# Reciprocals of softmax sums: spread by VectorE and turned by one transpose, in place of narrow products

## The chip, the cores and the metric

The kernel runs on one core of a Trainium2 chip. The metric is the device time of one execution in microseconds. Profiles are one execution each, recorded by the hardware profiler.

## What is computed

A block with two layers: each is a gated cross-attention to a context, followed by a gated feed-forward part. x has 16 batch rows of 100 tokens with 512 features; the context has 16 rows of 722 tokens with 384 features. Everything is float32. The part that matters here is the attention, once with 16 heads of 32 features (attention 0), once with 8 heads of 64 (attention 1):

```python
q = (query @ Wq + bq).reshape(B, Nq, H, D).transpose(0, 2, 1, 3)
k = (key_value @ Wk + bk).reshape(B, Nkv, H, D).transpose(0, 2, 1, 3)
v = (key_value @ Wv + bv).reshape(B, Nkv, H, D).transpose(0, 2, 1, 3)
attn = jnp.einsum('bhqd,bhkd->bhqk', q, k) * scale
attn = jax.nn.softmax(attn, axis=-1)
x = jnp.einsum('bhqk,bhkd->bqhd', attn, v).reshape(B, Nq, Cq)
return x @ Wo + bo
...
x = x + jnp.tanh(g_xattn[0]) * _L0_xattn_ref(_layernorm(x, axis=-1), ctx_768, ...)
x = x + jnp.tanh(g_ffn[0]) * _L0_ffn_ref(_layernorm(x, axis=-1), ...)
x = x + jnp.tanh(g_xattn[1]) * _L1_xattn_ref(_layernorm(x, axis=-1), ctx_768, ...)
x = x + jnp.tanh(g_ffn[1]) * _L1_ffn_ref(_layernorm(x, axis=-1), ...)
```

The first feed-forward part is a mixture of eight experts, the second has quantized weights. Neither is touched by the change.

## The kernel before

The kernel goes through attention 0, routing and experts, attention 1 and the quantized feed-forward part one after the other. Both attentions are the class `Attention`, with D = 32 or 64 features a head.

**Chunks.** Within an attention the work goes by batch row b (16) and by slice m of 128 features (4). One such pair, 64 in an attention, is called a chunk here; it holds G = 128 / D heads, that is four in attention 0 and two in attention 1. A chunk passes through these steps:

- `scores`: the products of queries and keys, tile `ps_s` (100 queries by 361 keys, two halves), line 315. VectorE negates them out of PSUM and takes the row minimum as it goes (`ns`, L338 with four heads in two parts, L325 with two heads); with four heads `extremes` (L348) joins the halves.
- `softmax`: ScalarE's exponentials (`pr`, L357), which also sum each row into `sums`.
- `turn`: TensorE transposes the probabilities of a pair of heads, four 100x128 blocks into one bank `ps_t` (L374), three banks a turn. The three are copied to `pT` by ScalarE (L381) or VectorE (L383), alternating by `(m + pair + q) % 2`. Four heads have two turns a chunk (turn 0 and turn 1), two heads one.
- `attend`: the reciprocal of `sums` (`rinv`, L390); the narrow products `ps_r` (L393), one for each head, whose weights are one column of `rinv` repeated D times and whose moving operand is the identity, so that `ps_r` holds each head's reciprocals along the queries in all its D feature rows; the copy `rb` of it (L401); the weighted sums of the values `ps_pv` (L406); and the product of `ps_pv` with `rb` into `tT` (L413). It comes one chunk later than the chunk's turns.

Between these stand "units" of other work for TensorE, one bank each: keys (`ps_k`, L181) and values (`ps_v`, L203) of the next batch row, queries (`ps_q`, L275), input transposes (`ps_tr`, L129), output projections (`ps_y`, L419), and in attention 0 the experts' `ps_logits` (L567).

**What sets the order.** TensorE's order is written out by hand in `run`. In step i it is: `scores` of the next chunk (part 0), `attend` of the chunk before, some units, turn 0 of this chunk, some units, and with four heads also `scores` part 1 of the next chunk, turn 1, and the rest of the units. The order on VectorE, ScalarE and GpSimd is set by a scheduler from the program's dependencies and its own costs.

**Buffers.** [...] `ps_s` takes four of them, and all the rest (`ps_k`, `ps_v`, `ps_q`, `ps_tr`, `ps_y`, `ps_logits`, `ps_t`, `ps_r`, `ps_pv`) share the pool `ps_m` of four banks. A tile of this pool gets a bank when the tile that held it has been copied out. `rinv` and `rb` have two buffers each.

Of the kernel before, what the change touches and what calls it, by code (L numbers as in the profile page):

```python
# [8 lines left out]
F32 = mybir.dt.float32  # L9
# [7 lines left out]
P = 128  # L17
B, T, C = 16, 100, 512
# [31 lines left out]
def bcast(ap, *shape):  # L50
    return ap.to_broadcast(list(shape))
# [6 lines left out]
def tiles_for(b):  # L58

    return [i for i in range(NTT) if (i * P + rows_of(i) - 1) // T == b]  # L60
# [72 lines left out]
class Attention:  # L133
# [232 lines left out]
    def turn(self, b, m, pair):  # L366
# [16 lines left out]
                nc.vector.tensor_copy(to, ps)  # L383
        self.pT[b, m, pair] = t

    def attend(self, b, m):
        nc, D, G = self.net.nc, self.D, self.G

        rinv = self.p2.tile([T, G], F32, tag="rinv", name="rinv")
        nc.vector.reciprocal(rinv, self.sums[b][:, m * G : (m + 1) * G])  # L390
        ps_r = self.ps_m.tile([P, T], F32, tag="mm", name="ps_r")
        for j in range(G):
            nc.tensor.matmul(  # L393
                ps_r[j * D : (j + 1) * D, :],
                bcast(rinv[:, j : j + 1], T, D),
                self.net.ident[:T, :T],
                start=True,
                stop=True,
            )
        rb = self.p2.tile([P, T], F32, tag="rb", name="rb")  # L400
        nc.vector.tensor_copy(rb, ps_r)  # L401
        ps = self.ps_m.tile([P, T], F32, tag="mm", name="ps_pv")
        for c in range(NS):
            n = P if c < NS - 1 else SL
            for j in range(G):
                nc.tensor.matmul(  # L406
                    ps[j * D : (j + 1) * D, :],
                    self.v[b][:n, c, m * P + j * D : m * P + (j + 1) * D],
                    self.pT[b, m, j // 2][:n, j % 2 * NS + c, :],
                    start=(c == 0),  # L410
                    stop=(c == NS - 1),
                )
        nc.vector.tensor_tensor(self.tT[:, m, b * T : (b + 1) * T], ps, rb, ALU.mult)  # L413
# [18 lines left out]
    def run(self, given, after_project=None):  # L432


        parts = 2 if self.G == 4 else 1
        steps = [(b, m) for b in range(B) for m in range(KC)]
        last_tile = lambda g: ((g + 1) * GT - 1) // P
        extra = {i: [] for i in range(len(steps) + 40)}
        for g in range(1, B // GB):
            at = 4 * KC * (g - 1)  # L440
            for n, i in enumerate(range(last_tile(g - 1) + 1, last_tile(g) + 1)):
                extra[at + 2 + n].append((self.query_input, i))
            for m in range(KC):
                extra[at + 7 + 2 * m].append((self.queries, g, m))
        for b in range(B):
            for i in tiles_for(b):
                at = (b + 1) * KC + 1
                extra[at].append((self.project, i))
                for later, *unit in after_project(i) if after_project else ():
                    extra[at + later].append(tuple(unit))  # L450
        todo = [u for b in range(1, B) for u in self.keys_and_values(b)]
        for i, (b, m) in enumerate(steps):
            if m == 0 and b + 2 < B and b + 2 not in self.cxs:
                self.load_ctx(b + 2)

            upto = max(0, min(len(todo), int(3.5 * (i + 1) - 2)))
            units = extra[i] + todo[given:upto]
            given = max(given, upto)
            nxt = steps[i + 1] if i + 1 < len(steps) else None
            if nxt:  # L460
                self.scores(*nxt, 0)
            if i:
                self.attend(*steps[i - 1])
            n = len(units)
            cut = [0, (n + 1) // 2, n] if parts == 1 else [0, (2 * n + 4) // 5, (3 * n + 4) // 5, n]
            for f, *a in units[cut[0] : cut[1]]:
                f(*a)
            self.turn(b, m, 0)
            for f, *a in units[cut[1] : cut[2]]:
                f(*a)  # L470
            if parts == 2:
                if nxt:
                    self.scores(*nxt, 1)
                self.turn(b, m, 1)
                for f, *a in units[cut[2] :]:
                    f(*a)
            if nxt:
                self.softmax(*nxt)
        self.attend(*steps[-1])
        for i in range(len(steps), len(steps) + 40):  # L480
            for f, *a in extra[i]:
                f(*a)
# [976 lines left out]
```

## Time and profile before

| | us |
|---|---|
| median of 3 runs | 2925.89 (2925.71 to 2926.7) |
| the profiled execution's own time | 2935.15 |
| its span, from first to last instruction | 2933.4 |
| TensorE (PE) busy | 2819.8 |
| VectorE (DVE) busy | 869.2 |
| ScalarE (ACT) busy | 855.2 |
| the narrow products ps_r: 512 matmul records in attention 0, 256 in attention 1 | busy 24.2 and 25.3 |
| the reciprocals at L390, 128 | busy 21.8 |
| the copies rb at L401, 128 | busy 32.9 |

How to read it: a float32 product leaves two matmul records, a transpose one. Records of matmuls overlap and their ends are modelled, so the distance from one start to the next tells what a product costs; "busy" counts overlaps once. PEld is the loading of weights, which mostly runs beside matmuls. In tables by shape, "128x400 f32<-128x400 f32" is what is written and what is read. "idle before <-" names what ended the idle time of an engine ahead of a group. Attention 0's chunks run from about 85 to 975 us of the span, attention 1's from about 1730 to 2500.

### The profile page before, as it was taken

What the parts mean: (1) busy time and instruction counts of PE and PEld (TensorE: products, weight loads), DVE (VectorE), ACT (ScalarE), POOL (GpSimd) and SP (SyncE); (2) the same over time, 40 slices, a digit from 0 to 9 for tenths busy, and PEclk for the clock granted to TensorE, in tenths of its full rate; (3) what the DMA queues carried; (4) which work ended last, traced back from release to release, by engine and by line L of the source; (5) the groups of instructions that cost most, each with busy time, mean ns of one, the idle gap of its engine ahead of it and who ended that gap; (6) DMA issues with size and microseconds to landing.
All of it is one profiled execution on the core that took longest, in us unless ns stands there. A gap on an engine that the chain in (4) does not pass through costs nothing. (4 is left out here: it accounts for less than half of the span.)

```text
span 2933.4 us, 42386 instructions
## 1 busy us (share of the span) xinstructions
PE 2819.8 (96%) x17968; PEld 1746.7 (60%) x17968; DVE 869.2 (30%) x2565; ACT 855.2 (29%) x1710; POOL 149.2 (5%) x170
## 2 busy tenths in 40 slices
PE   7999999999999989999999979999999999499999
PEld 3555555555556578887888645555555556245543
DVE  2544444444445400000000163232232223410000
ACT  1544444454455300000000123333333333111110
POOL 2000000000000000000000140000000000210000
PEclk9999999999999999999999979999999999799999
DMA  4000010000000388889888420000000000700000
GB/s 155 16 16 16 18 37 24 16 27 32 16 27 21 137 320 315 314 323 318 312 316 313 153 64 31 16 31 16 16 31 16 31 16 1 225 8 11 11 11 13
DMA packets 131240, 278.10 MB, mean 95 GB/s; under 512 B 6880, under 2 KB 6880, under 8 KB 130528
## 3 DMA queue, kind: packets, MB, share of 16 engines
q1 hardware_dynamic: 111168, 231.19, 22.4%
q10 hardware_dynamic: 15328, 29.14, 3.0%
q0 software_dynamic: 4544, 14.95, 1.4%
q8 instruction: 145, 2.38, 0.3%
q14 instruction: 55, 0.45, 0.1%
HBM read 260.31 MB, written 14.94 MB: 94 GB/s over the span
## 5 line engine op out<-in xcount | busy, mean ns | idle before, releaser
L203 PE MATMUL ps_v<-wv_a,ctx_a 128*128 128x512 f32 (+1 forms) x1152 | 524.5, 600 | 7.6 <-ACT v_a L210 5.2
L181 PE MATMUL ps_k<-ctx_a,wk_a 128*128 128x361 f32 x1536 | 510.0, 477 | 14.4 <-DMA ctx_a<-in_ctxT 10.9
L774 PE MATMUL ps_h<-xT,w 128*128 128x128 f32 x3712 | 421.0, 276 | 0.9 <-DVE xT L762 0.9
L774 PEld LDWEIGHTS ps_h<-xT,w 128*128 128x128 f32 x3712 | 418.4, 193 | 1.8 <-DVE xT L762 1.3
L181 PEld LDWEIGHTS ps_k<-ctx_a,wk_a 128*128 128x128 f32 x1536 | 283.2, 192 | 174.1 <-issue 28.3
L203 PEld LDWEIGHTS ps_v<-wv_a,ctx_a 128*128 128x128 f32 (+1 forms) x1152 | 204.6, 185 | 243.8 <-issue 228.2
L338 DVE TENSOR_SCALAR_CACHE_REDUCE ns<-ps_s 100x361 f32<-100x361 f32 x512 | 246.9, 529 | 208.2 <-PE ps_s L315 185.8
L374 PEld LDWEIGHTS ps_t<-ident,pr_a 100*128 100x128 f32 x2304 | 214.0, 141 | 81.0 <-issue 41.7
L357 ACT ACTIVATE pr_a<-ns,extremes 100x722 f32<-100x722 f32 x256 | 227.2, 889 | 78.9 <-DVE extremes L348 78.9
L374 PE MATMUL ps_t<-ident,pr_a 100*128 100x100 f32 x2304 | 237.1, 252 | 1.5 <-DVE rb L401 1.1
L383 DVE COPY pT<-ps_t 128x400 f32<-128x400 f32 x288 | 163.7, 572 | 251.6 <-PE ps_t L374 245.6
L315 PE MATMUL ps_s<-kT_a,qT_a 32*100 32x361 f32 (+1 forms) x1536 | 213.6, 501 | 9.9 <-DVE ns L325 7.4
L210 ACT COPY v_a<-ps_v 128x512 f32<-128x512 f32 x192 | 111.3, 581 | 340.7 <-PE ps_v L203 340.4
L794 PE MATMUL ps_o<-w,midT 128*128 128x512 f32 x464 | 203.9, 592 | 0.0
L977 PE MATMUL ps_z<-ffn_w,y_ffn 128*128 128x512 f32 (+1 forms) x416 | 195.5, 607 | 5.4 <-ACT y_ffn L967 5.4
L325 DVE TENSOR_SCALAR_CACHE_REDUCE ns<-ps_s 100x722 f32<-100x722 f32 x128 | 111.4, 907 | 278.2 <-PE ps_s L315 278.2
L959 PE MATMUL ps_y<-hT,ffn_w 128*128 128x384 f32 (+1 forms) x512 | 188.9, 513 | 0.0
L381 ACT COPY pT<-ps_t 128x400 f32<-128x400 f32 x288 | 141.5, 492 | 158.8 <-PE ps_t L374 149.4
L315 PEld LDWEIGHTS ps_s<-kT_a,qT_a 32*100 32x100 f32 (+1 forms) x1536 | 73.7, 162 | 141.6 <-issue 92.6
L406 PE MATMUL ps_pv<-pT,v_a 128*32 128x100 f32 (+3 forms) x4608 | 156.6, 249 | 0.4 <-DVE pT L383 0.3
L785 DVE TENSOR_TENSOR midT<-silu,ps_h 128x512 f32<-128x512 f32 x58 | 39.9, 688 | 386.0 <-PE ps_h L774 386.0
L959 PEld LDWEIGHTS ps_y<-hT,ffn_w 128*128 128x128 f32 x512 | 98.2, 195 | 90.8 <-issue 52.9
(149 smaller groups left out, 1804.8 us busy)
## 6 DMA issues: line engine op xcount, KB each, us to landing
w<-in_L_ffn_w SPq DMA_DIRECT2D x116, 1024.0 KB, 7.1
w<-in_L_ffn_wo SPq DMA_DIRECT2D x29, 2048.0 KB, 11.0
ctx_a<-in_ctxT SPq DMA_DIRECT2D x30, 1083.0 KB, 5.2
q<-in_L_ffn_fc_q SPq DMA_DIRECT2D x8, 1024.0 KB, 10.8
s<-in_L_ffn_fc_scales ACTq DMA_DIRECT2D x8, 1024.0 KB, 12.4
rows<-ot ACTq DMA_DIRECT2D x29, 256.0 KB, 8.7
x<-in_x ACTq DMA_DIRECT2D x1, 3072.0 KB, 20.6
xn_d<-xn_moe ACTq DMA_DIRECT2D x12, 256.0 KB, 2.0
```

The source lines that it names most:

```text
L181: nc.tensor.matmul(ps, self.wk[:, k, m * P : (m + 1) * P], self.cxs[b][:, k, c * SH : (c + 1) * SH], start=(k == 0), stop=(k == KK - 1),)
L203: nc.tensor.matmul(ps[:n], self.cxs[b][:, k, c * P : c * P + n], self.wv[:, k, :], start=(k == 0), stop=(k == KK - 1),)
L315: nc.tensor.matmul(pss[n // 2][:, n % 2, :SH], self.qT[g][j * D : (j + 1) * D, m, q], self.kT[b, m][j * D : (j + 1) * D, c * SH : (c + 1) ...
L338: nc.vector.tensor_scalar(self.negated[b, m][j][:, part * SH : (part + 1) * SH], pss[j // 2][:, j % 2, :SH], -1.0, BIG, ALU.mult, ALU.min, ...
L357: nc.scalar.activation(self.prob(b, h)[:, :S], ns, AF.Exp, bias=self.nmax[b][:, h : h + 1], scale=-1.0, accum_out=self.sums[b][:, h : h + 1],)
L374: nc.tensor.transpose(ps[:, i, :], self.prob(b, m * G + 2 * pair + j)[:, c * P : (c + 1) * P], self.net.ident[:T, :T],)
L383: nc.vector.tensor_copy(to, ps)
L406: nc.tensor.matmul(ps[j * D : (j + 1) * D, :], self.v[b][:n, c, m * P + j * D : m * P + (j + 1) * D], self.pT[b, m, j // 2][:n, j % 2 * NS ...
L774: nc.tensor.matmul(ph[:, f, :], w[:, n, k, f * P : (f + 1) * P], self.xT[j][:, k, :], start=(k == 0), stop=(k == KC - 1),)
L794: nc.tensor.matmul(po, self.midT[j, f // 4][:, f % 4, :], w[:, f, :], start=(f == 0), stop=(f == KF - 1),)
L959: nc.tensor.matmul(ps[:, :nt], w1[f // nf][:, k, f % nf * P : (f % nf + 1) * P], hT[:, k, :nt], start=(k == 0), stop=(k == KC - 1),)
L977: nc.tensor.matmul(z[j][:n], y[:, j * P : j * P + n], w2[f // nf][:, f % nf, :], start=(f == 0), stop=(f == NF - 1),)
```

## The change

The reciprocals become a step of their own, `inverse_sums`. VectorE takes the reciprocal of each sum D times over, by reading the sums through a broadcast access pattern, so that `rinv` is 100 x 128 and not 100 x 4 or 100 x 2. One transpose of this tile by TensorE then gives `ps_r`, in place of the four or two narrow products; the copy to `rb` stays. In `run` the step stands behind turn 1 and ahead of the last units with four heads, and at the end of the units with two heads; so it belongs to the current chunk, and `attend`, which comes in the next step, finds `rb` made.

```diff
+    def inverse_sums(self, b, m):
+
+        nc, D, G = self.net.nc, self.D, self.G
+        rinv = self.p2.tile([T, G, D], F32, tag="rinv", name="rinv")
+        sums = self.sums[b][:, m * G : (m + 1) * G]
+        nc.vector.reciprocal(rinv, bcast(sums.unsqueeze(2), T, G, D))
+        ps_r = self.ps_m.tile([P, T], F32, tag="mm", name="ps_r")
+        nc.tensor.transpose(ps_r, rinv.rearrange("p g d -> p (g d)"), self.net.ident[:T, :T])
+        self.rb = self.p2.tile([P, T], F32, tag="rb", name="rb")
+        nc.vector.tensor_copy(self.rb, ps_r)
+
     def attend(self, b, m):
         nc, D, G = self.net.nc, self.D, self.G
-
-        rinv = self.p2.tile([T, G], F32, tag="rinv", name="rinv")
-        nc.vector.reciprocal(rinv, self.sums[b][:, m * G : (m + 1) * G])
-        ps_r = self.ps_m.tile([P, T], F32, tag="mm", name="ps_r")
-        for j in range(G):
-            nc.tensor.matmul(
-                ps_r[j * D : (j + 1) * D, :],
-                bcast(rinv[:, j : j + 1], T, D),
-                self.net.ident[:T, :T],
-                start=True,
-                stop=True,
-            )
-        rb = self.p2.tile([P, T], F32, tag="rb", name="rb")
-        nc.vector.tensor_copy(rb, ps_r)
+        rb = self.rb
         ps = self.ps_m.tile([P, T], F32, tag="mm", name="ps_pv")
...
                 self.turn(b, m, 1)
+                self.inverse_sums(b, m)
                 for f, *a in units[cut[2] :]:
                     f(*a)
+            else:
+                self.inverse_sums(b, m)
             if nxt:
                 self.softmax(*nxt)
```

## The prediction

> **What bounds the kernel now.** I read the busy shares first, then the stages, then single chunks in the timeline. A chunk is one 128-feature slice of one batch row: 64 chunks of four heads in attention 0, 64 of two heads in attention 1. The first part of the page and two stretches of the table by stage (span, then busy us of PE, PEld, DVE, ACT, POOL, then clock):
>
> ```profile
> PE 2819.8 (96%) x17968; PEld 1746.7 (60%) x17968; DVE 869.2 (30%) x2565; ACT 855.2 (29%) x1710; POOL 149.2 (5%) x170
> ...
> 85.00:975.00 890.00, 887.11 (x7723) 520.63 (x7720) 424.23 (x1556) 442.53 (x917) 22.73 (x25) 1.00 0.07 25
> ...
> 1700.00:2500.00 800.00, 788.78 (x4562) 455.82 (x4563) 256.13 (x646) 281.28 (x571) 35.54 (x34) 0.98 0.07 23
> ```
>
> The two attentions, where the change lies, are PE from end to end (99.7% and 98.6%); DVE is under half busy. So a microsecond that PE issues or waits there is a microsecond of the end, and work on DVE costs only where PE waits for it. The timeline of PE around two chunks shows what the narrow products cost (start, length):
>
> ```profile
> 651.79 0.87 PE L315 MATMUL ps_s<-kT_a,qT_a 32*100 32x361 f32 x8
> 652.59 0.38 PE L393 MATMUL ps_r<-ident,rinv 100*32 100x100 f32 x8
> 652.79 1.22 PE L406 MATMUL ps_pv<-pT,v_a 128*32 128x100 f32 x48
> ...
> 2047.75 0.39 PE L393 MATMUL ps_r<-ident,rinv 100*64 100x100 f32 x4
> 2047.98 1.20 PE L406 MATMUL ps_pv<-pT,v_a 128*64 128x100 f32 x24
> ```
>
> Ends are modelled, so starts count: from ps_r to ps_pv is 0.20 us in attention 0 and 0.23 in attention 1 (0.195 and 0.222 in nearly all records), not 0.38, and far from 4 x 261 ns: four column strips run side by side.
>
> **What the Trainium skill says.** "TensorEngine Tiling (Array Packing)", Key Properties: changing the tiling mode drains the array. The trace agrees: a score product after a key product starts 0.395 us after it, a key product after a key product 0.302. "TensorE: Matmul & The Clock Gate", Architectural detail: the queue pulls weight loads ahead of running matmuls. The trace agrees by its exception: where a key product's first weight load waited for a copy (642.31 us), its group of 12 took 3.84 us instead of 3.76, so a wait that ends late costs 0.08 us of open load on top. "VectorE: DVE Perf Modes", First, the fixed hardware budget: the reciprocal is an iterative divide with a repeat count of 8. The rows by shape agree:
>
> ```profile
> L390 DVE RECIPROCAL rinv<-sums_a 100x4 f32<-100x4 f32 x64 | 11.2, 175 | 128.5 <-ACT pr_a L357 128.5
> ...
> L108 DVE RECIPROCAL rstd<-rstd 128x1 f32<-128x1 f32 x5 | 0.7, 147 | 0.0
> ...
> L708 DVE RECIPROCAL probs<-first 128x13 f32<-128x13 f32 x1 | 0.2, 241 | 0.0
> L108 DVE RECIPROCAL rstd<-rstd 128x9 f32<-128x9 f32 x1 | 0.2, 216 | 0.1
> ```
>
> From 1 to 13 elements is (241 - 147) / 12 = 7.8 ns an element, where a DVE copy out of PSUM grows by (257 - 159) / 92 = 1.1 ns (128x100 against 128x8).
>
> **The change part by part.**
>
> *Narrow products out, a transpose in (PE).* The first load behind the score products is open whoever comes: the first round of ps_r takes 0.109 us (two heads: 0.136), a later round 0.086 to 0.09. With ps_r gone, ps_pv inherits that, 0.02 and 0.05. Saved: 64 x (0.195 - 0.02) + 64 x (0.222 - 0.05) = 22.2 us. The transpose has the shape of a ps_t one, 100x128 weights and 100 columns; those start 0.086 us apart (12 in 1.03). Added: 128 x 0.086 = 11.0 us. Net **-11.2**. If ps_pv inherits nothing it is -15.6.
>
> *A bank wait (PE, attention 0).* ps_m has four banks. Before, a chunk took them as ps_r, ps_pv, units, three ps_t (turn 0), units, three ps_t (turn 1), units. After, ps_r comes right behind turn 1, so turn 1 and ps_r hold all four, and the next unit (a ps_k or ps_v) must take a bank of the turn just made. The changed program's order confirms it: that product waits for the ACT copy of this turn's first ACT-copied bank, in nearly every chunk. An odd chunk (pT copied by DVE, ACT, DVE) and an even one (ACT, DVE, ACT), in the timeline:
>
> ```profile
> 646.95 1.25 PE L374 MATMUL ps_t<-ident,pr_a 100*128 100x100 f32 x12
> 647.95 0.49 ACT L381 COPY pT<-ps_t 128x400 f32<-128x400 f32 x1 [1.12 <-PE ps_t L374]
> 648.03 3.83 PE L181 MATMUL ps_k<-ctx_a,wk_a 128*128 128x361 f32 x12
> ...
> 659.70 1.25 PE L374 MATMUL ps_t<-ident,pr_a 100*128 100x100 f32 x12
> 660.36 1.12 ACT L381 COPY pT<-ps_t 128x400 f32<-128x400 f32 x2 [0.78 <-PE ps_t L374]
> 660.79 2.01 PE L181 MATMUL ps_k<-ctx_a,wk_a 128*128 128x361 f32 x6
> ```
>
> Odd: the copy ends at 648.44; a waiting PE starts 0.055 later (as at 655.80 to 655.856), 648.50; behind the transpose the unit would start at 648.03 + 0.09 = 648.12. Wait 0.37, plus the open load 0.08. Even: the first copy ends 660.36 + 0.49 = 660.85, so 660.91 against 660.88: 0.03 + 0.08. The same distances recur all through the stage, 31 odd and 30 even chunks with a unit there: 31 x 0.45 + 30 x 0.11 = **+17.3**. Ends: +12.4 without open loads, +20 if each is 0.05 longer. Everything behind that product on PE's queue moves with it; no later wait takes it up, as PE has hardly any in this stage. In attention 1 the transpose stands at the chunk's end, next to ps_pv in the rotation as before: no such wait.
>
> *The reciprocal (DVE).* 128 elements at 7.8 ns: 147 + 127 x 7.8 = 1.14 us; I take 1.1, against 0.18. The low end is the price of a copy, 0.28. That is +0.93 x 128 = 119 us of DVE. In the changed order it keeps its place, at the chunk's start behind the exponentials and ahead of the row maxima (the order has it well before turn 1, so the transpose itself does not wait for it). What is queued behind it:
>
> ```profile
> 653.66 0.18 DVE L390 RECIPROCAL rinv<-sums_a 100x4 f32<-100x4 f32 x1 [3.66 <-ACT pr_a L357]
> ...
> 655.54 0.26 DVE L401 COPY rb<-ps_r 128x100 f32<-128x100 f32 x1
> 655.90 0.26 DVE L413 TENSOR_TENSOR tT_a<-ps_pv,rb 128x100 f32<-128x100 f32 x1
> ```
>
> Four maxima, then rb (which leaves this place: -0.36, the distance of the two starts), then the product that frees ps_pv's bank. It comes 0.93 - 0.36 = 0.6 us later. In most chunks its bank is asked for over 1 us later and the delay is hidden; at ten places, those with short units (logits, ps_tr), PE takes the bank 0.09 us after the product's end and would wait about 0.55 more, at five more with 0.4 to 0.55 us of room about 0.15: 10 x 0.55 + 5 x 0.15 = **+6**. At the low price it is -2.5, since rb's wait goes. In attention 1 DVE idles from 2050.9 to 2054.1 in such a chunk, which covers 1.1 us: nothing; without that cover it would be 0.9 a chunk.
>
> *rb's copy, 0.26 us, 128 times.* Attention 0: behind turn 1's copies and the `extremes` that release the exponentials, so it delays neither. Attention 1: ahead of the maxima, in the 0.8 us and more that the score products take. Nothing, and no DMA and nothing on POOL or SP is moved; if it did stand ahead of the exponentials it would cost up to 0.26 where PE waits for them, and PE doesn't.
>
> *The two starts.* In chunk 0 of each attention PE has nothing between the exponentials and ps_r, and the long reciprocal lies open: about 1 us each, **+2**.
>
> Sum: -11.2 + 17.3 + 6 + 2 = **+14 us**. On the profiled execution's own time (span 2933.4 and 1.75 around it, 2935.15) that is 2949; that execution lies 9.3 us above the median of the runs, 2925.89. The steps are differences of PE time at the same clock (1.00 and 0.98), so I put them on the median: **2939**.
>
> **The rivals.** A measurement of this kernel can tell 0.2%, 5.9 us, from no change.
>
> - *Faster: fewer PE instructions, and the bank wait isn't there.* For it: 256 of 384 products go, and the waits list has almost no PE wait for copies in this stage. It decides if the bank is free by 648.12 in such a chunk instead of 648.44, so that -11.2 stands with 0 to 8 beside it: 2915 to 2923. Against it: the order names the copy waited for, and the copy's times are in the trace. The sum turns below zero where bank waits and reciprocal together cost under 11 us.
> - *No change: the reciprocal is priced like a copy.* Then -2.5 for +6, and 0.5 for the starts: +4, 2930. Against it are the five shapes of reciprocal above, small ones though.
> - *Much slower: DVE late in each chunk.* Score products of part 1 take their banks 1.4 us after the maxima that free them. A reciprocal of 2 us would pass this, and PE would wait some 0.5 us in each of 64 chunks: +32 more, 2970; at 1.6 us some 10 more. The slope speaks against it, extrapolated tenfold.
> - *The transpose waits for the reciprocal behind turn 1's copies*, which would be 3 us a chunk: excluded by the order.
>
> **How the numbers follow.** My case 0.60 (2933 to 2948 by the ends above), no change 0.18, faster 0.12, much slower 0.10. Slower than 0.2%: 0.60 + 0.10 = 0.70; within: 0.18; faster: 0.12. The range takes in my case and the cheap reciprocal and leaves out the fast rival and the far part of the slow one: 2926 to 2951.
>
> **What would show it.** In the profile after: ps_r as 128 matmul records instead of 768, about 0.086 us apart from their neighbours; ps_pv 0.80 us (1.39) behind the score products; a group ps_k or ps_v <- ACT pT in PE's waits, some 60 times, 10 us and more in all; the reciprocal at 1.0 to 1.2 us and DVE near 990 us busy; attention 1 shorter by about 5 us and attention 0 longer by 18 to 20. I'm wrong if the unit behind ps_r starts 0.09 us after it, or if the reciprocal takes under 0.5 us.

## The result and the profile after

The changed kernel takes 2943.89 us (median of 6 runs) against 2926.95 us before (6 runs): ratio 1.0051, 95% interval 1.0038 to 1.0064. A second set of runs gave 2940.95 against 2927.13, ratio 1.0046 (1.0032 to 1.0059). It is slower by 14 to 17 us; the forecast was 13 slower than the median.

The busy line of the page and the two stretches of the table by stage, in the changed kernel:

```profile
PE 2815.0 (96%) x17328; PEld 1741.6 (59%) x17328; DVE 959.1 (33%) x2565; ACT 855.5 (29%) x1710; POOL 148.5 (5%) x170
...
85.00:975.00 890.00, 878.11 (x7075) 508.95 (x7064) 455.90 (x1529) 435.44 (x902) 22.64 (x25) 1.00 0.07 25
...
1700.00:2500.00 800.00, 781.86 (x4327) 452.39 (x4325) 313.59 (x658) 281.25 (x572) 44.50 (x42) 0.98 0.08 24
```

PE has 640 records fewer, and the kernel is slower: in attention 0's stretch PE is now busy for 878.11 of 890 us where it was 887.11. Idle time has come in where there was hardly any. DVE has 90 us more.

The measure that I use from here on is the distance from the first to the last `ps_pv` record of an attention. Two profiled executions of one program agree in it within 0.5 us, while the stretches between the attentions differ by several us from one to the next (from PE's first product to the first `ps_pv` the first profile of before takes 81.0 us and the second 76.6, which is half of why the first lay 9 us above the median). Before: 881.5 and 881.5 us in attention 0, 759.5 and 759.1 in attention 1. After: 898.1 and 897.7, and 755.4 and 755.1. So **attention 0 is 16.4 us longer and attention 1 is 4.0 shorter**, 12 of the 14 to 17 us. The rest lies outside these stretches; what is known of it stands with the granted clock below.

The same odd and even chunk as in the prediction, some 5 us later, in the timeline of the changed kernel (start, length, engine, line):

```profile
652.91 0.49 ACT L381 COPY pT<-ps_t 128x400 f32<-128x400 f32 x1 [1.12 <-PE ps_t L374]
653.00 0.25 PE L393 MATMUL ps_r<-ident,rinv 100*128 100x100 f32 x1
653.45 3.00 PE L181 MATMUL ps_k<-ctx_a,wk_a 128*128 128x361 f32 x9 [0.21 <-ACT pT L381]
...
665.69 1.12 ACT L381 COPY pT<-ps_t 128x400 f32<-128x400 f32 x2 [0.78 <-PE ps_t L374]
666.12 0.25 PE L393 MATMUL ps_r<-ident,rinv 100*128 100x100 f32 x1
666.24 2.09 PE L181 MATMUL ps_k<-ctx_a,wk_a 128*128 128x361 f32 x6
```

Odd: the unit comes 0.45 us behind `ps_r` (0.086 of work and 0.37 of waiting), right after the ACT copy ends at 653.40. Even: 0.12 behind, of which 0.03 is waiting. All 60 pairs of `ps_r` and a unit in the stage lie at one of these two distances, 30 at 0.113 to 0.116 and 30 at 0.456 to 0.462.

The late product, in the same trace:

```profile
658.61 0.95 DVE L391 RECIPROCAL rinv<-sums_a 100x128 f32<-100x128 f32 x1 [3.49 <-ACT pr_a L357]
...
661.24 0.26 DVE L411 TENSOR_TENSOR tT_a<-ps_pv,rb 128x100 f32<-128x100 f32 x1
...
661.55 0.65 PE L374 MATMUL ps_t<-ident,pr_a 100*128 100x100 f32 x5 [0.41 <-DVE tT_a L411]
```

The reciprocal holds up four maxima and the product behind them, and a bank of `ps_t` waits for that product, here for 0.41 us. The reciprocal's row by shape, for its price:

```profile
L391 DVE RECIPROCAL rinv<-sums_a 100x128 f32<-100x128 f32 x128 | 121.8, 952 | 180.4 <-ACT pr_a L357 180.4
```

### The profile page after: what moved, and what is told of

Same layout as the page of the kernel before. It is cut to its first block, busy times and chain, and to the rows that moved or that the text cites. A ratio compares the mean times of both kernels' runs of the same rounds, so it can differ in the third digit from the quotient of the medians.

```text
span 2936.0 us, 41108 instructions
## 1 busy us (share of the span) xinstructions
PE 2815.0 (96%) x17328; PEld 1741.6 (59%) x17328; DVE 959.1 (33%) x2565; ACT 855.5 (29%) x1710; POOL 148.5 (5%) x170
## 5 line engine op out<-in xcount | busy, mean ns | idle before, releaser
L203 PE MATMUL ps_v<-wv_a,ctx_a 128*128 128x512 f32 (+1 forms) x1152 | 525.6, 601 | 12.3 <-ACT v_a L210 5.1
L391 DVE RECIPROCAL rinv<-sums_a 100x128 f32<-100x128 f32 x128 | 121.8, 952 | 180.4 <-ACT pr_a L357 180.4
L404 PEld LDWEIGHTS ps_pv<-pT,v_a 128*32 128x32 f32 (+3 forms) x4608 | 135.0, 120 | 68.4 <-issue 46.8
## 6 DMA issues: line engine op xcount, KB each, us to landing
w<-in_L_ffn_wo SPq DMA_DIRECT2D x29, 2048.0 KB, 10.3
```

The source lines that it names most:

```text
L203: nc.tensor.matmul(ps[:n], self.cxs[b][:, k, c * P : c * P + n], self.wv[:, k, :], start=(k == 0), stop=(k == KK - 1),)
L404: nc.tensor.matmul(ps[j * D : (j + 1) * D, :], self.v[b][:n, c, m * P + j * D : m * P + (j + 1) * D], self.pT[b, m, j // 2][:n, j % 2 * NS ...
```

## The experiments

**Theory:** in attention 0 two costs outweigh PE's saving: the *bank* that `ps_r` holds beside turn 1's three, so that the next unit waits for an ACT copy, and the *late product* behind the long reciprocal. **Rivals:** the reciprocal is the whole cost and the place costs nothing; the transpose itself is dear on PE (a change of mode); or the runs only had a lower granted clock (the share of its full speed that TensorE was given, the third last column of the stage tables).

All that ran (us; stretches from first to last `ps_pv`; of attention 0's stretch, how long its trace has TensorE at half clock; the sum against the second profile of before, 1640.6; the median against before's median beside the same runs):

| kernel | attention 0 | of it at half clock | attention 1 | sum | median | ratio (95%) |
|---|---|---|---|---|---|---|
| before, again | 881.5 | 0 | 759.1 | 0 | -0.6 | 0.9998 (0.9990 to 1.0006) |
| changed, again | 897.7 | 3.4 | 755.1 | +12.1 | +13.8 | 1.0046 (1.0032 to 1.0059) |
| ps_r ahead of scores | 892.0 | 13.7 | 755.4 | +6.8 | +9.3 | 1.0028 (1.0019 to 1.0038) |
| short reciprocal | 893.9 | 6.8 | 755.2 | +8.4 | +8.4 | 1.0027 (1.0015 to 1.0039) |
| both of these | 880.6 | 3.4 | 754.2 | -5.9 | -3.2 | 0.9988 (0.9982 to 0.9995) |
| end of chunk, long | 887.5 | 10.2 | 755.7 | +2.5 | 0.0 | 1.0003 (0.9995 to 1.0012) |
| end of chunk, short | 879.3 | 6.8 | 755.2 | -6.2 | -4.7 | 0.9982 (0.9974 to 0.9990) |
| long reciprocal only | 894.1 | 6.8 | 760.2 | +13.7 | +13.9 | 1.0044 (1.0031 to 1.0058) |
| all chunks even | 892.5 | 10.2 | 754.8 | +6.8 | +8.9 | 1.0027 (1.0018 to 1.0036) |
| all chunks odd | 905.3 | 0 | 755.9 | +20.6 | +22.5 | 1.0075 (1.0062 to 1.0088) |
| attention 1 only | 881.5 | 0 | 755.7 | -3.4 | -3.4 | 0.9986 (0.9978 to 0.9994) |
| new place only | 897.5 | 0 | 768.8 | +25.7 | +27.3 | 1.0091 (1.0076 to 1.0105) |

The medians follow the two stretches within 3 us in every row. The **granted clock** is not the main cause: beside the second set fourteen runs of before with a mean clock of 0.979 took 2926.2 to 2932.0 us, 2928.3 on the mean, and the changed kernel at 0.979 took 2938.1 (2937.8 in the first set). That is 10 us more at the same clock, where this rival allows under 3. But the clock isn't nothing: the changed kernel's other runs had 0.976 to 0.978, and the remaining 4 to 7 us go together with that.

Within attention 0 it disturbs the measure too, which I had missed. In its traces TensorE is at half clock for short stretches. One of them, in the kernel "end of chunk, long", first as a row of the stage table, with the clock 0.50, then in PE's timeline:

```profile
475.90:479.30 3.40, 3.40 (x9) 1.90 (x7) 0.98 (x2) 0.42 (x1) 0.00 (x0) 0.50 0.19 70
```

```profile
476.06 3.60 PE L181 MATMUL ps_k<-ctx_a,wk_a 128*128 128x361 f32 x6
479.60 0.87 PE L315 MATMUL ps_s<-kT_a,qT_a 32*100 32x361 f32 x8
...
481.48 2.01 PE L181 MATMUL ps_k<-ctx_a,wk_a 128*128 128x361 f32 x6
483.33 1.02 PE L203 MATMUL ps_v<-wv_a,ctx_a 128*128 128x512 f32 x2
```

Six key products take 3.54 us there, from start to next start, and 1.85 right after, so a stretch of 3.4 us costs 1.7. Two of them lie in mid-attention in "ps_r ahead of scores" and in "end of chunk, long", one in "long reciprocal only" and in "all chunks even", all kernels with the long reciprocal; the rest of that column lies at the end of attention 0, in the last two chunks. What sets them off was not tried.

**The changed kernel and the one before, again.**

> The changed kernel once more, on the chip and beside the runs of the kernel before that the next three share. Theory (bank wait and late product): attention 0 about 11 us longer than before, attention 1 about 5 us shorter, 2937 to 2945 us in all, ratio 1.002 to 1.006. Rival 'granted clock': its times follow its granted clock and not its work; then a run of it and one of the kernel before with the same clock differ by under 3 us.

> The kernel before once more, for what two profiled executions of one program differ by. The first one was 8 us above the median of the other runs. If that is scatter outside the chunks: first to last ps_pv of attention 0 again 881.5 within 0.5 us and of attention 1 759.5 within 0.5, with the difference ahead of the first ps_pv (81.0 us there, 77 to 79 in the other kernels' profiles) and between the stages. If the chunks themselves scatter, these stretches differ by several us and can't be compared between kernels.

Measured: the first two rows. The time in all and attention 1 are as expected, and so is before; attention 0 is 16 us longer, where the expectation still had about 11. The chunks repeat, what lies between them scatters. Of PE's waits in attention 0 (total us, times, longest; the totals count from modelled ends, so they show about half of a start-to-start wait):

```profile
PE ps_v L203 <- ACT pT L381: 3.1, 15, 0.2
PE ps_k L181 <- ACT pT L381: 3.1, 15, 0.2
PE ps_t L374 <- DVE tT_a L411: 2.1, 6, 0.4
PE ps_r L393 <- DVE rinv L391: 1.8, 1, 1.8
PE ps_v L203 <- DVE tT_a L411: 1.6, 3, 0.5
```

The first two are the bank wait in 30 odd chunks, the third and the fifth the late product.

**Is it the bank? The engine of one copy.**

```diff
-            if (m + pair + q) % 2:
+            if ((m if self.G == 2 else 0) + pair + q) % 2:
```

> The changed kernel, only the engines of the copies of ps_t in attention 0: in every chunk as in the even ones, so that turn 1 is copied by ScalarE, VectorE, ScalarE (the choice no longer depends on m). The work, its places and the long reciprocal stay. Theory of the bank wait: behind ps_r the unit waits for turn 1's first ACT copy, which in odd chunks is the copy of the second bank, 0.34 us later than in even ones; with the first bank copied by ACT everywhere that goes: 31 x 0.34 = 10.5 us off the stretch from first to last ps_pv of attention 0, 897.9 to 886 to 890; hardly anything <- ACT pT in PE's waits. Rival 'the place costs something else' (order of the queues, an open load behind ps_r, a change of mode): 895 to 900.

With a 1 for the 0, all chunks are odd:

> The same the other way round: in every chunk of attention 0 as in the odd ones, so that turn 1 is copied by VectorE, ScalarE, VectorE. Theory: the 30 even chunks with a unit behind ps_r now wait 0.34 us more too: 30 x 0.34 = 10.2 us on top, 905 to 910; ps_k and ps_v <- ACT pT about twice as long in PE's waits. Rival 'the place costs something else': 895 to 900.

Measured: 905.3 with all chunks odd, as expected; 892.5 with all even, half of what was expected. PE's waits in attention 0, first all odd, then all even (where no wait for an ACT copy of `pT` is listed any more):

```profile
PE ps_k L181 <- ACT pT L381: 7.1, 34, 0.2
PE ps_v L203 <- ACT pT L381: 5.4, 26, 0.2
```

```profile
PE ps_t L374 <- DVE tT_a L411: 3.4, 7, 0.8
PE ps_r L393 <- DVE rinv L391: 1.9, 3, 1.0
```

Twice as long in one, gone in the other, by nothing but which engine copies a bank: the **bank wait is shown**, and with it that the place has a price that isn't the reciprocal's. From `ps_r` to the unit, summed over the stage, it is 17.1 us in the changed kernel and 6.8 in "all even", so the 10.3 us did go. About half came back: 1.7 us in a chunk at half clock, 0.9 in the last two chunks, where the half clock lasts 6.8 us instead of 3.4, and the rest as other waits. PE arrives earlier, and the product, which hasn't become any earlier, is waited for longer (3.4 against 2.1 us in this view).

**Another place: ahead of the score products of part 1.**

```diff
             if parts == 2:
+                self.inverse_sums(b, m)
                 if nxt:
                     self.scores(*nxt, 1)
                 self.turn(b, m, 1)
-                self.inverse_sums(b, m)
```

> In attention 0 the step inverse_sums goes from behind turn 1 to ahead of the score products of part 1, nothing else. Theory: turn 1 and ps_r no longer hold all four banks of ps_m when the next unit comes, so the group ps_k or ps_v <- ACT pT leaves PE's waits; ps_r to unit, 31 x 0.37 us and 30 x 0.03 us, goes, and some open loads; the late product stays. Attention 0 shorter than in the changed kernel by 9 to 14 us, that is within 3 us of before; in all 8 to 14 us below the changed kernel. Rival 'the reciprocal is the whole cost' (its 0.95 us on VectorE delays the copies and products, the place costs nothing): as the changed kernel, within 3 us. Rival 'granted clock': as the changed kernel at the same clock.

Measured: 5.7 us off attention 0 where 9 to 14 were expected, 4.6 off the median. PE's waits in attention 0:

```profile
PE ps_t L374 <- DVE tT_a L411: 4.8, 7, 0.9
PE ps_r L393 <- DVE rinv L391: 4.3, 2, 3.0
```

The ACT waits are gone as expected. In their place stand 2.7 us more for the product and 2.5 more for the reciprocal itself: `ps_r` comes earlier in the chunk, and in the last two chunks, where few units or none are left ahead of it, PE sits 3.2 and 1.4 us before it. Two chunks at half clock add 3.4 us. My expectation had left out all three; without the last two chunks and without these 3.4 us, attention 0 is 11.7 us shorter than in the changed kernel.

**The short reciprocal.**

```diff
-        nc.vector.reciprocal(rinv, bcast(sums.unsqueeze(2), T, G, D))
+        few = self.p2.tile([T, G], F32, tag="few", name="few")
+        nc.vector.reciprocal(few, sums)
+        nc.vector.tensor_copy(rinv, bcast(few.unsqueeze(2), T, G, D))
```

> The place of the changed kernel, but the reciprocal is taken of the 100 x 4 or 100 x 2 sums (0.15 to 0.18 us) and a copy spreads it to 100 x 128 (0.26 us): 0.45 us on VectorE in place of 0.95. Theory: the bank wait stays at 12 us and more, only the product that frees the bank of ps_pv comes 0.5 us earlier, so the waits of ps_t and ps_v for that product go: attention 0 shorter by 4 to 6 us than in the changed kernel, still 5 to 7 longer than before. Rival 'the reciprocal is the whole cost': most of the 11 us go and PE's saving shows, attention 0 at or below before. Rival 'granted clock': no change at the same clock.

> The two edits together: ps_r ahead of the score products of part 1, and the short reciprocal with a spreading copy. Theory: both costs go and PE's saving is left: attention 0 about 4 to 7 us shorter than before (22 narrow-product us less 11 of transposes, half of it in each attention), attention 1 about 5 shorter; in all 9 to 13 us below before, 2913 to 2918, which beats both. Rival 'the reciprocal is the whole cost': as the short reciprocal alone. Rival 'granted clock': as before at the same clock.

Measured: 893.9 alone. The half microsecond is worth 3.8 us, just under the 4 to 6 expected (5.4 by the median), and the place more: attention 0 stays 12.4 us above before, not 5 to 7, as the expectation had taken 11 for the whole excess. Its two instructions, from the rows by shape, cost 0.43 us together against 0.95:

```profile
L393 DVE COPY rinv<-few 100x128 f32<-100x128 f32 x128 | 33.2, 259 | 4.3
...
L392 DVE RECIPROCAL few<-sums_a 100x4 f32<-100x4 f32 x64 | 11.3, 176 | 121.3 <-ACT pr_a L357 121.3
```

Both edits together: 880.6, only 0.9 below before in attention 0 instead of 4 to 7 (PE still waits 3.8 us for `rinv` in two places), and 3.2 us below before in the median instead of 9 to 13.

**A place without a unit behind it: the end of the chunk, as in attention 1.** Two kernels, with the long and with the short reciprocal.

```diff
-                self.inverse_sums(b, m)
                 for f, *a in units[cut[2] :]:
                     f(*a)
+                self.inverse_sums(b, m)
```

> The changed kernel with inverse_sums at the very end of the chunk's units in attention 0 too, as it stands in attention 1; the reciprocal stays long (0.95 us). Measure: the stretch from the first to the last ps_pv of attention 0, 881.5 us before, 897.9 in the changed kernel, 893.9 with the short reciprocal, 892.0 with ps_r ahead of the score products. Theory (two costs, the bank that ps_r holds beside turn 1, and the late product): only the late product is left, 882 to 888. Rival 'ps_r costs a bank wherever it stands', which the run with ps_r ahead of the score products speaks for: 891 or more, with ps_t or ps_pv waiting for a bank. Rival 'the reciprocal is the whole cost': 896 to 899.

> The same place at the end of the units, with the short reciprocal and the spreading copy. Theory: both costs gone, PE's saving shows: stretch of attention 0 877 to 881 us, attention 1 about 755 (759.5 before); in all 5 to 10 us below before, ratio 0.9965 to 0.9985, at least as fast as the two edits tried together with the other place. Rival 'ps_r costs a bank wherever it stands': 884 and more, no faster than before. Rival 'the reciprocal is the whole cost': the place makes no difference, so as the short reciprocal behind turn 1, 893.9.

Measured: 887.5 and 879.3, both in the theory's band and in neither rival's; the median of the second is 4.7 us below before, just short of the 5 to 10. This makes two tables of two by two, for attention 0 and for the medians against before:

| | long, attention 0 | short, attention 0 | difference | long, median | short, median | difference |
|---|---|---|---|---|---|---|
| behind turn 1 | 897.7 | 893.9 | 3.8 | +13.8 | +8.4 | 5.4 |
| end of chunk | 887.5 | 879.3 | 8.2 | 0.0 | -4.7 | 4.7 |
| difference | 10.2 | 14.6 | | 13.8 | 13.1 | |

Neither "only the reciprocal" nor "only the place" gives these: both costs are there. By the profiled executions each cost seems to hide 4.4 us of the other; by the medians **the two costs add up**, within what these runs can tell. The difference is mostly clock. The profile of "end of chunk, long" is one of five executions at 2931.8 to 2934.2 us, while the other eight took 2924.1 to 2927.3, and its trace has the two half-clock stretches in mid-attention, 3.4 us, which the other three of this table don't have. PE's waits with the end of the chunk, the long reciprocal first:

```profile
PE ps_t L374 <- DVE tT_a L411: 4.2, 7, 0.9
```

```profile
PE ps_t L374 <- DVE tT_a L413: 1.6, 4, 0.4
```

**The long reciprocal alone,** in the kernel before.

```diff
-        rinv = self.p2.tile([T, G], F32, tag="rinv", name="rinv")
-        nc.vector.reciprocal(rinv, self.sums[b][:, m * G : (m + 1) * G])
+        rinv = self.p2.tile([T, G, D], F32, tag="rinv", name="rinv")
+        sums = self.sums[b][:, m * G : (m + 1) * G]
+        nc.vector.reciprocal(rinv, bcast(sums.unsqueeze(2), T, G, D))
...
-                bcast(rinv[:, j : j + 1], T, D),
+                rinv[:, j, :],
```

> The kernel before, with its place and its narrow products, but the reciprocal 100 x 128 long (the weights of the narrow products are then read from the long tile). It asks what the long reciprocal costs by itself. Theory: the product behind it on VectorE comes 0.77 us later, with rb still ahead of it, so PE waits for ps_pv's bank at the ten places with short units, and somewhat at others: stretch of attention 0 887 to 893 us against 881.5; attention 1 759 to 760, hidden. Rival 'the reciprocal is the whole cost': 897 or more. Rival 'VectorE has room, the reciprocal costs nothing': 881 to 883.

Measured: 894.1, 12.6 us more, a little above the 6 to 12 that I gave (1.7 of it is a chunk at half clock), and 1 in attention 1. PE's waits in attention 0:

```profile
PE ps_t L374 <- DVE rb L402: 6.0, 9, 1.1
PE ps_t L374 <- DVE tT_a L414: 1.6, 4, 0.4
```

In the old place the long reciprocal also delays `rb`, and `rb` frees `ps_r`'s own bank. So 0.77 us more of reciprocal costs 12.6 us there, while 0.52 us more costs 3.8 where the change puts it. That it moves `rb` out from between the reciprocal and the product is the likely reason; it was not tried by itself.

**The place alone,** with the narrow products and the short reciprocal, and **attention 1 alone.**

```diff
-        rinv = self.p2.tile([T, G, D], F32, tag="rinv", name="rinv")
+        rinv = self.p2.tile([T, G], F32, tag="rinv", name="rinv")
...
-        nc.vector.reciprocal(rinv, bcast(sums.unsqueeze(2), T, G, D))
+        nc.vector.reciprocal(rinv, sums)
...
-        nc.tensor.transpose(ps_r, rinv.rearrange("p g d -> p (g d)"), self.net.ident[:T, :T])
+        for j in range(G):
+            nc.tensor.matmul(ps_r[j * D : (j + 1) * D, :], bcast(rinv[:, j : j + 1], T, D), ...)
```

> The new place alone: inverse_sums stands where the change puts it, but takes the short reciprocal and spreads it by the narrow products of before, no transpose and no spreading copy. Theory: the place alone makes attention 0 longer. In odd chunks the unit waits for the same ACT copy, so it starts at the same time whatever ps_r took; in even ones the narrow products' 0.195 us lies open instead of 0.086: stretch of attention 0 892 to 896 us, near the short reciprocal's 893.9. Rival 'the transpose is what costs PE' (a change of mode): 881 to 886. Attention 1 close to before, 758 to 760.

> The change in attention 1 alone; attention 0 keeps the narrow products and their place. Theory: attention 0 as before, 881.5, attention 1 as in the changed kernel, 755 to 755.7 against 759.3: about 4 us below before, 2922 to 2924, ratio 0.998 to 0.999. Rival 'granted clock' (the transposes or the longer VectorE work lower it): no faster than before.

Attention 1 alone came out as expected, 3.4 us below before. The place alone missed, on the dear side: 897.5 and, in attention 1, 768.8 where I had expected no change. PE's timeline at the end of a chunk of attention 1, in this kernel and then in the changed one:

```profile
2070.12 2.01 PE L181 MATMUL ps_k<-ctx_a,wk_a 128*128 128x361 f32 x6
2072.06 0.39 PE L394 MATMUL ps_r<-ident,rinv 100*64 100x100 f32 x4
2072.38 1.46 PE L315 MATMUL ps_s<-kT_a,qT_a 64*100 64x361 f32 x8
```

```profile
2063.24 2.01 PE L181 MATMUL ps_k<-ctx_a,wk_a 128*128 128x361 f32 x6
2065.08 0.25 PE L393 MATMUL ps_r<-ident,rinv 100*128 100x100 f32 x1
2065.26 1.46 PE L315 MATMUL ps_s<-kT_a,qT_a 64*100 64x361 f32 x8
```

Between key and score products the narrow ones come 1.94 us behind the group of six instead of 1.84, and are followed after 0.32 instead of 0.18. The rival "the transpose is what costs PE" is refuted: without it, and with the short reciprocal, attention 0 is as long as in the changed kernel. The Trainium skill, "TensorEngine Tiling (Array Packing)", Key Properties, says that a change of the tiling mode drains the array. The distances of the starts agree, though they can't show the reason. In attention 0 the step into the narrow products is dearer: 0.179 us behind a transpose, where from transpose to transpose it is 0.086, 63 times. In attention 1 the step into them, 0.396 us behind a key product, is not new, as the score products behind a key product took 0.396 before. New is the step out of them: 0.179 us to the score products, against 0.079 to the weighted sums in the place of before, 61 times and so 6 us; another 4 are the first load of `ps_pv`, which now lies open. Together they are about the 9.7. So in this place the transpose is the cheaper one, 893.9 against 897.5 us in attention 0 and 755.2 against 768.8 in attention 1, both with the short reciprocal; what makes the change slow in attention 0 is the place and the long reciprocal.

## Why the prediction was right

The direction, the cause and the time held. By its steps, for attention 0 from the starts in the second profile of the changed kernel against the second of before:

- *Narrow products out, a transpose in.* Foreseen there: 64 x 0.175 saved, 5.5 added, -5.7. Measured: the records of `ps_r` before, 12.3 us, went; 63 x 0.086 = 5.4 came; `ps_pv` inherited 0.022 a chunk: **-5.5**. In attention 1 -4.0 against -5.5: `ps_pv` inherited 0.07 there, not 0.05 (4.6 us over the 64 chunks), and the rest is as foreseen.
- *The bank wait.* Foreseen +17.3. Measured: 18.0 us from `ps_r` to the next group less 5.4 of work, 12.6, and open loads of 4.2 in the key and value groups (0.07 each): **+16.8**, and the two kernels with all chunks odd or even moved it as the step says.
- *The reciprocal.* Foreseen ten waits of 0.55 us for the product and five of 0.15, +6. Measured: nine waits, six inside a turn (0.43 to 0.57) and three ahead of `ps_v` (0.68), 5.1 in all; the five short ones aren't there; and 2.0 us of waits behind `rb`, ahead of and inside a turn's `ps_t`, are gone, which I had counted for the low price only: **+3.1**. The price, 1.1 us foreseen, is 0.952, that is (952 - 147) / 127 = 6.3 ns an element where I had carried 7.8 over from the small shapes; DVE's 959 us, against 990 foreseen, is the same error.
- *The starts.* Foreseen about 1 us each. The start of attention 0 costs 0.5, that of attention 1 0.1. The wait that I hadn't named is at the end of attention 0: in the last chunk but one the reciprocal does not keep its place ahead of the row maxima but stands behind those of the last chunk and a copy, and PE waits **1.9** us for it (1.3 in the first profile).

The sum, -5.5 + 16.8 + 3.1 + 1.9 = 16.3, stands against 16.2 measured; what isn't listed nearly cancels (the last chunk's transposes come 0.17 us apart in that profile, as TensorE is at half clock from 977.8 us on for 3.4 us: +1.4, and some small terms of the other sign). So the mis-sized term was the late product, 3 us too dear, and attention 1's saving, 1.5 too large; they offset each other in part in the forecast. That the total came so near is in part luck: the 1.9 and the 1.4 at the end of attention 0 were not foreseen, nor were the 2 to 5 us of the median outside the attentions. The rival "the bank wait isn't there" fell at its own point: the bank came free at 653.40, where PE could have used it at 653.09. "Priced like a copy" was refuted by the row: 952 ns. At 0.95 us the maxima were not late either, so the much slower case did not come.

In "end of chunk, short" attention 0 is only 2.2 us shorter than before, where PE's saving alone would give 5.5. The missing part lies at the end: up to the last two chunks it is 5.1 us shorter, and from there on 2.7 longer, with 6.8 us at half clock and a listed wait of 1.3 us for `rinv`. What stays open is what sets off the half clock, there and in mid-attention.

The best version found is that one, 2922.15 us against 2926.85 before: ratio 0.9982 (0.9974 to 0.9990), the change's own saving without most of its two costs.

## What to carry to other kernels

Before a small step is moved, count the buffers of its pool at the new place: one more tile behind a group that fills the pool turns the next instruction into a wait for the youngest copy, and the names in the waits list say which. A remedy tried alone can show only part of its worth: `ps_r` ahead of the scores took 4.6 us off the median, the short reciprocal 5.4, both together 17.1. A table of two by two tells more than two single edits, but it needs the medians and the clock beside it: here two short stretches at half clock, in one profiled execution, looked like two causes that cover each other. Where a small operation spreads a few values over many elements, price the operation per element: a reciprocal of 4 elements and a copy took 0.43 us where the reciprocal of 128 took 0.95.

## What the runs showed of the hardware

- The 100x128 reciprocal through a broadcast took 951 to 952 ns in every kernel that had it, 6.3 ns an element beyond the first, while a copy of the same shape through the same broadcast took 259. The Trainium skill, "VectorE: DVE Perf Modes", First, the fixed hardware budget, calls the reciprocal an iterative divide; what that costs an element is seen in these rows.
- Narrow products in column strips cost more next to other neighbours: those of two heads took 0.23 us up to the next group between score products and weighted sums (2047.75 to 2047.98), and 0.32 between key and score products. With the weighted sums' open load attention 1 grew by 9.7 us over its 64 chunks.
- A copy's engine alone, with the work unchanged, moved the kernel by 13.7 us in the median, and attention 0 from 892.5 to 905.3, between "all even" and "all odd".
- TensorE ran at half clock for stretches of 3.4 us and multiples of it, and one of these in a busy chunk cost 1.7 us (six key products in 3.54 us instead of 1.85). The clock of a whole stage doesn't show one: the changed kernel's stage from 85 to 975 us reads 1.00 and holds 3.4 us of half clock, from 971.6 us on.
